# Layer 1 of a two-layer graph network: how a group's rows are finished, where head 0's and head 3's row sums are made, and which tiles take the log form

## The chip, the cores and the metric

The kernel runs on one core of one Trainium2 chip. The metric is the device time of one execution in microseconds, as the median of the runs; the profile is one further execution, taken by the hardware profiler. The core has five engines that run their own queues in order and wait for one another by semaphores: TensorE (PE in the profile; PEld is its weight load), VectorE (DVE), ScalarE (ACT), GpSimd (POOL) and SyncE (SP), which here only issues transfers.

## The reference

Two layers over 4096 nodes with 512 features. Layer 0 is a dense attention layer; the change does not touch it. Layer 1, with eight heads of 64 features, is this (the connectivity is the 0/1 matrix `adj`, added as it is):

```python
h = jnp.maximum(_layernorm(x, axis=-1), 0.0)
data1 = (h @ W.T + b).reshape(N, H, D)              # N, H, D = 4096, 8, 64
src = jnp.einsum('nhd,xhd->nh', data1, src_proj)
trg = jnp.einsum('nhd,xhd->nh', data1, trg_proj)
e = src.T[:, :, None] + trg.T[:, None, :]
e = jnp.where(e >= 0, e, 0.01 * e)
e = e + connectivity[None, :, :]
scores = jax.nn.softmax(e, axis=-1)
out = jnp.einsum('hnm,hmd->hnd', scores, data1.transpose(1, 0, 2))
x = x + out.transpose(1, 0, 2).reshape(N, H * D)
```

## The kernel before

Layer 1 works through eight groups. A group is a block `b` of 1024 target rows and a half `g` of four heads. Each group takes 32 steps; step `m` handles the source nodes 128m to 128m+127, which lie on the partitions, against the 1024 rows along the free axis. A head's unnormalised scores for one step are a 128x1024 product, called `pr` and numbered by head 0 to 3 within the half. The exponential of a leaky sum is written as a maximum of two factors times the exponential of `adj`, so that most products are one VectorE instruction.

The work of a step goes round the engines like this. SP loads a 128x1024 tile `e` of `adj` (L700, three buffers). ScalarE makes `ex` from it in PSUM (L718, one buffer) for heads 0, 1, 2, makes `e3` with a bias (L728) for head 3, and a rectified row `rl` for head 0 (L746). VectorE makes the four products in the order 3, 0, 1, 2 (`weigh`, L757 for head 0 and L760 for the others). The products of heads 1, 2 and 3 have two buffers each, those of head 0 three.

In `BY_LOG` steps head 0 is done in another form: ScalarE writes `lg` (L735), a GpSimd DMA adds `adj` to it (L736), and ScalarE's exponential gives the product (L743), so that VectorE has three products instead of four. These are the special tiles; before, they are steps 17, 21, 25 and 29.

TensorE's `gather` multiplies the products by the node values (L792). Each head's 64 features are split in two pieces of 32 columns, so four matmuls, each on its own 32 columns of the array, run side by side into the `pv` tiles. Row sums (the softmax denominators) go to `dn`, whose four quarters of 32 partitions are again four column tiles. Heads 1 and 2 have row sums on TensorE in every step. Head 0 has them on TensorE only in the steps that are not in `BY_DMA`; otherwise a GpSimd DMA adds the product to one of two accumulators `acc00`, `acc01` in SBUF (L774 to L776). Head 3's products are added up by a GpSimd `tensor_tensor` into `acc3` (L767, L769) for steps 0 to 30. A row sum of a single head 0 step fills only two of the four column tiles, so `side` switches between the two halves, and the next such step can use the other two. In the last step of a group TensorE adds the head 3 product of step 31 and the three accumulators, each once (L807 to L814). After that ScalarE copies `pv` to `os` (L821).

The group's end is spread over the next group's first steps by the generator `finish`: copy `dn` in step 0, turn the denominators in step 1 (L831), reciprocal `rd` on VectorE in step 2 (L835), and then one 128-row tile of the group per step: two transposes on TensorE (L847) into the one `pt` buffer, four scaled ScalarE copies in the next step (L871), and, for every second tile, a GpSimd DMA that adds the residual `x1` (L874) and three steps later a SP DMA to the output (L877).

The order of work around all this is the loop at L964 to L975: for each program step `s` it calls each stage for step `s + ahead` and then one `next(ending)`. Every engine's queue follows that order.

```python
stages = ((load, 3), (logs, 5), (exps, 1), (weigh, 1), (factors, 2), (scale, 2), (gather, 0))
```

So while TensorE gathers step s, VectorE weighs s+1 and SP loads s+3. The broadcast rows `z` of the next group (four DMAs of 512 KB, L695) and `u` are issued inside `load`. The last group is finished by `finish_last`, which keeps everything on chip.

Of the kernel before, what the change touches and what calls it, by code (L numbers as in the profile page):

```python
# [8 lines left out]
FP = mybir.dt.float32  # L9
AF = mybir.ActivationFunctionType  # L10
ALU = mybir.AluOpType
# [4 lines left out]
P = 128  # L16
# [12 lines left out]
def kernel(  # L29
# [15 lines left out]
    nc = tc.nc  # L45
    N, F = x.shape
    H, D = 8, 64
    HG, WL = 4, 1024
    WT = WL // P
    NT = N // P  # L50
# [12 lines left out]
    x1 = dram.tile([N, F], FP, name="x1")  # L63
# [36 lines left out]
    with tc.tile_pool(name="w0", bufs=1) as wp, tc.tile_pool(name="a0", bufs=2) as ap_, tc.tile_pool(  # L100
        name="a0s", bufs=8
# [144 lines left out]
    with tc.tile_pool(name="mx", bufs=1) as mxp, tc.tile_pool(name="b_a", bufs=6) as adjp, tc.tile_pool(  # L246
        name="b_e", bufs=4
    ) as esp, tc.tile_pool(name="b_m", bufs=2) as mkp, tc.tile_pool(name="b_s", bufs=2) as sp, tc.tile_pool(
        name="b_p", bufs=6, space=PSUM
# [56 lines left out]
        for n in range(-6, len(items)):  # L306
# [3 lines left out]
            if n >= 0:  # L310
                i, j, t = items[n]
# [9 lines left out]
    with tc.tile_pool(name="c_a", bufs=11) as adjp, tc.tile_pool(name="c_b", bufs=4) as ebp, tc.tile_pool(  # L321
        name="c_e", bufs=9
    ) as etp, tc.tile_pool(name="c_w", bufs=3) as wkp, tc.tile_pool(name="c_t", bufs=3) as atp, tc.tile_pool(
        name="c_m", bufs=2
    ) as mxp, tc.tile_pool(name="c_o", bufs=4) as iop, tc.tile_pool(name="c_s", bufs=2) as sp, tc.tile_pool(
        name="c_p", bufs=1, space=PSUM
    ) as p_o, tc.tile_pool(name="c_q", bufs=3, space=PSUM) as p_t, tc.tile_pool(
        name="c_r", bufs=1, space=PSUM
# [3 lines left out]
        src, pts, aj, mks, ex, at = {}, {}, {}, {}, {}, {}  # L332
# [112 lines left out]
        left, scale = [], {}  # L445
# [145 lines left out]
        pt = p_t.tile([P, BL], FP, name="pt")  # L591
# [44 lines left out]
    HV = WL // BL  # L636
    JT = BL // P
    Q = P // 4
    BY_LOG = (17, 21, 25, 29)
    BY_DMA = [m for m in range(2, NT - 5) if m % 4 != 1]  # L640

    with tc.tile_pool(name="p", bufs=2) as prp, tc.tile_pool(name="rl", bufs=2) as rlp, tc.tile_pool(
        name="io1", bufs=3
# [48 lines left out]
        def zload(i, k):  # L692
            b, g = groups[i]
            zs_[i, k] = (zp1 if i % 2 else zp0).tile([P, WL], FP, name=f"z{k}")
            nc.sync.dma_start(zs_[i, k], row_bcast(z_d, WL, (g * HG + k) * N + b * WL))  # L695

        def load(i, m):
            b, g = groups[i]
            e = ep.tile([P, WL], FP, name="e")
            nc.sync.dma_start(e, adj_t[m * P:(m + 1) * P, b * WL:(b + 1) * WL])  # L700
            ra[i, m] = e
            if i + 1 < len(groups) and m == 28:
                us[i + 1] = usp.tile([P, WL], FP, name="u")
                b, g = groups[i + 1]
                nc.sync.dma_start(us[i + 1], row_bcast(u_d, WL, g * N + b * WL))
            if i + 1 < len(groups) and m in (20, 22, 24, 26):
                zload(i + 1, ORDER[(m - 20) // 2])

        def scale(i, m):

# [38 lines left out]
        def weigh(i, m, order=ORDER):  # L749
            h = groups[i][1] * HG  # L750
            x_ = ex.pop((i, m))
            for k in order:
                if (i, m, k) in pr:
                    continue
                w = prp.tile([P, WL], FP, name=f"pr{k}", bufs=3 if k == 0 else 2)
                if k == 0:
                    nc.vector.scalar_tensor_tensor(w, rl.pop((i, m)), ngd_m[:, h // HG, m:m + 1], x_,  # L757
                                                   op0=ALU.subtract, op1=ALU.mult)
                else:
                    nc.vector.scalar_tensor_tensor(w, zs_[i, k], g_m[:, h + k, m:m + 1],  # L760
                                                   e3.pop((i, m)) if k == 3 else x_,
                                                   op0=ALU.max, op1=ALU.mult)
                pr[i, m, k] = w
            w = pr[i, m, 3]
            if m == 1:
                acc[i, 3] = acp.tile([P, WL], FP, name="acc3", bufs=1)
                nc.gpsimd.tensor_tensor(acc[i, 3], pr[i, 0, 3], w, ALU.add)  # L767
            elif 1 < m < NT - 1:
                nc.gpsimd.tensor_tensor(acc[i, 3], acc[i, 3], w, ALU.add)  # L769
            if m in BY_DMA:  # L770
                n = BY_DMA.index(m)
                if n < 2:
                    acc[i, 0, n] = acp.tile([P, WL], FP, name=f"acc0{n}", bufs=1)
                    nc.gpsimd.dma_start(acc[i, 0, n], pr[i, m, 0])  # L774
                else:
                    nc.gpsimd.dma_start(acc[i, 0, n % 2], pr[i, m, 0], accum_op=ALU.add)  # L776

        def gather(i, m):
            b, g = groups[i]
            last = m == NT - 1  # L780
            if m == 0:
                pv[i] = ([[p_v.tile([P, BL], FP, name=f"pv{c}{q}") for q in range(HV)] for c in range(2)],
                         p_v.tile([P, BL], FP, name="dn"))
            v, dn = pv[i]
            by_pe = [u for u in range(NT) if u not in BY_DMA]
            side = sum(u < m for u in by_pe) % 2
            for c, pair in enumerate(((3, 0), (1, 2))):
                for q in range(HV):
                    for r in (side, 1 - side):
                        k = pair[r]  # L790
                        for c0 in range(0, D, Q):
                            nc.tensor.matmul(v[c][q][r * D + c0:r * D + c0 + Q, :],  # L792
                                             va[:, m, g * HG + k, c0:c0 + Q],
                                             pr[i, m, k][:, q * BL:(q + 1) * BL], start=(m == 0), stop=last)

            def den(r, w, src, q, **fl):
                nc.tensor.matmul(dn[r * Q:r * Q + w.shape[1], :], w, src[:, q * BL:(q + 1) * BL], **fl)  # L797

            for r in (side, 1 - side):
                for q in range(HV):  # L800
                    hk = g * 2 + r
                    den(r * HV + q, d0_m[:, hk, m, :] if m else d0_0[:, hk, :], pr[i, m, r + 1], q,
                        start=(m == 0), stop=False)
            if m in by_pe:
                for q in range(HV):
                    den(side * HV + q, zo[:, 1 - side:3], pr[i, m, 0], q, start=False, stop=False)
            if last:  # L807
                for q in range(HV):
                    den(HV + q, zo[:, 1:3], pr[i, m, 3], q, start=False, stop=False)
                for q in range(HV):  # L810
                    den(q, zo[:, 1:3], acc[i, 0, 1], q, start=False, stop=False)
                for r, a in enumerate((acc[i, 0, 0], acc[i, 3])):
                    for q in range(HV):
                        den(r * HV + q, zo[:, 1:3], a, q, start=False, stop=True)  # L814
            for k in range(HG):
                pr.pop((i, m - 1, k), None)
            if last:
                os_ = [[osp.tile([P, BL], FP, name=f"os{c}{q}") for q in range(HV)] for c in range(2)]
                for c in range(2):
                    for q in range(HV):  # L820
                        nc.scalar.copy(os_[c][q], v[c][q])  # L821
                late[i] = os_, dn
# [15 lines left out]
        def share(rd, t, r):  # L838
            q, j = divmod(t, JT)
            k = ORDER[r]  # L840
            e, r4 = (0, (k - 1) * HV + q) if k in (1, 2) else (1, (HV if k else 0) + q)
            return rd[:, j, e, r4:r4 + 1]
# [7 lines left out]
        def part(ap, i, t, n):  # L850

            b, g = groups[i]
            t += b * WT
            return ap[t * P:(t + n) * P, g * HG * D:(g + 1) * HG * D].rearrange("(j p) (h d) -> p j h d", p=P, h=HG)

        def finish(i):


            dens = denominators(i)
            os_ = next(dens)  # L860
            yield
            next(dens)
            yield
            rd = next(dens)
            pts, os2 = {}, {}
            for t in range(WT + 4):
                if 0 < t <= WT:
                    if t % 2:
                        o = iop.tile([P, 2, HG, D], FP, name="o")
                    for r, k in enumerate(ORDER):  # L870
                        nc.scalar.activation(o[:, (t - 1) % 2, k, :], pts[t - 1][:, r, :], AF.Copy,  # L871
                                             scale=share(rd, t - 1, r))
                    if t % 2 == 0:
                        nc.gpsimd.dma_start(o, part(x1, i, t - 2, 2), accum_op=ALU.add)  # L874
                        os2[t] = o
                if t - 3 in os2:
                    nc.sync.dma_start(part(out, i, t - 5, 2), os2[t - 3])  # L877
                if t < WT:
                    pts[t] = p_t.tile([P, HG, D], FP, name="pt")
                    turn(os_, t, pts[t])  # L880
                yield

        def finish_last(i):

# [5 lines left out]
            os_ = next(dens)  # L890
            pts = [p_v.tile([P, HG, D], FP, name=f"pv{c}{q}") for q in range(HV) for c in range(2)]
            xs = p_x.tile([P, 4, HG, D], FP, name="ex")
            pts += [xs[:, n, :, :] for n in range(4)]
            for t in range(4):
                turn(os_, t, pts[t])
            next(dens)
# [64 lines left out]
        factors(0, 1)  # L961
        scale(0, 1)

        stages = ((load, 3), (logs, 5), (exps, 1), (weigh, 1), (factors, 2), (scale, 2), (gather, 0))  # L964
        for s in range(len(steps)):
            for f, ahead in stages:
                if s + ahead < len(steps):
# [44 lines left out]
```

## Time and profile before

| what | value |
|---|---|
| median of 3 runs | 2971.45 us (2970.3 to 2971.49) |
| the profiled execution's own time | 2974.0 us |
| its span, first to last instruction | 2972.2 us |
| layer 1's first and last `pv` matmul | 1743.5 us, 2956.0 us |
| granted TensorE clock | 0.996 |
| one VectorE product, 128x1024 (L760 on `ex`) | 1272 ns mean |
| one GpSimd sum, 128x1024 (L769) | 2410 ns mean, 232 of them |
| DMA accumulations of head 0 (L774, L776) | 152, 512 KB each |

Layer 1 is the last 41% of the span. A table of the eight groups is part of the prediction. In such a table, the busy time of PE counts a matmul as busy from its start to a modelled end, and several matmuls run side by side, so a PE that is busy all the time does not mean that it has no free columns. For VectorE, ScalarE and GpSimd busy time is the time an instruction ran, waits inside the instruction included.

### The profile page before, as it was taken

Reading aid. Unit: us, or ns where it says so; the run is one execution under the profiler, and the core shown is the slowest. Engines: PE = TensorE matmul, PEld = TensorE weight load, DVE = VectorE, ACT = ScalarE, POOL = GpSimd, SP = SyncE. Lnnn points to the kernel's source line nnn. Section 1 sums busy time; section 2 is a strip of 40 time slices with the busy share of each in tenths; the row PEclk is TensorE's granted clock in tenths of the full one; section 3 lists DMA queues with packets and bytes.
Section 4 is the critical chain, followed back from the end, with each engine's and each line's share of the span. In section 5 each row is a group of like instructions: output and inputs, shape, how many; then the busy total and the mean of one; then the engine's idle time right before and its main releaser. Section 6 shows DMA issues by size and latency. Waiting matters only on the chain.

```text
span 2972.2 us, 43109 instructions
## 1 busy us (share of the span) xinstructions
PE 2930.7 (99%) x15371; PEld 1159.4 (39%) x15371; DVE 2522.1 (85%) x3596; ACT 1326.1 (45%) x1852; POOL 1376.0 (46%) x1042
## 2 busy tenths in 40 slices
PE   8999999999999999999999989999999999999998
PEld 4444444444444444444444423323222322232222
DVE  5434777778888888888897789999999999999998
ACT  2121111111122122122122368888777777777776
POOL 3401111113444444444443656575757575757574
PEclk9999999999999999999999999999999999999999
DMA  4205666667976675665553149696969696979795
GB/s 155 96 7 179 223 222 219 230 219 184 208 180 172 159 177 173 157 175 177 155 179 99 54 138 239 183 255 192 251 196 247 201 248 202 241 206 240 209 230 154
DMA packets 454056, 552.02 MB, mean 186 GB/s; under 512 B 261624, under 2 KB 287256, under 8 KB 453840
## 3 DMA queue, kind: packets, MB, share of 16 engines
q1 hardware_dynamic: 400816, 387.81, 42.2%
q0 software_dynamic: 51008, 157.51, 23.0%
q10 hardware_dynamic: 2016, 3.93, 0.4%
q8 instruction: 121, 1.98, 0.3%
q14 instruction: 95, 0.78, 0.1%
HBM read 409.47 MB, written 59.97 MB: 158 GB/s over the span
## 4 chain that ended last, share of the span: by engine, by line
PE 85%; DVE 6%; DMA 4%; ACT 2%; issue 2%; POOL 1%; SPq 0%; DVEq 0%; ACTq 0%; POOLq 0%
PE po L437 30%; PE pv L792 20%; PE pe L288 15%; PE dn L797 7%; DVE pr L760 5%; PE ps L159 4%; PE po L507 4%; PE pe L166 4%; DMA acc<-pr 2%; DMA e<-in_adj_t_dram 1%; DVE pr L757 1%; PE pt L847 1%; ACT e L728 1%; POOL acc L769 1%; ACT ex L718 0%
## 5 line engine op out<-in xcount | busy, mean ns | idle before, releaser
L792 PE MATMUL pv<-pr,sup 128*32 128x512 f32 x8192 | 1010.4, 595 | 10.3 <-POOL d_m L957 5.4
L437 PE MATMUL po<-sup,at 128*128 128x512 f32 x2048 | 886.7, 594 | 2.2 <-DVE at L407 2.2
L769 POOL TENSOR_TENSOR acc<-acc,pr 128x1024 f32<-128x1024 f32 x232 | 559.2, 2410 | 315.4 <-DVE pr L760 314.9
L760 DVE SCALAR_TENSOR_TENSOR pr<-z,g_m,ex 128x1024 f32<-128x1024 f32 x512 | 630.7, 1272 | 7.9 <-ACT ex L718 7.5
L437 PEld LDWEIGHTS po<-sup,at 128*128 128x128 f32 x2048 | 387.4, 190 | 480.7 <-issue 446.1
L417 POOL TENSOR_TENSOR racc<-racc,ex 128x512 f32<-128x512 f32 x240 | 358.3, 1493 | 390.7 <-ACT ex L401 389.0
L792 PEld LDWEIGHTS pv<-pr,sup 128*32 128x32 f32 x8192 | 288.5, 110 | 594.6 <-issue 528.2
L401 ACT ACTIVATE ex<-d 128x512 f32<-128x512 f32 x256 | 160.5, 630 | 664.7 <-DVE d L399 648.1
L288 PE MATMUL pe<-he_t,he_t 128*128 128x512 f32 x896 | 386.4, 592 | 0.0
L718 ACT ACTIVATE ex<-e 128x1024 f32<-128x1024 f32 x256 | 263.0, 1027 | 219.7 <-DVE pr L760 219.4
L760 DVE SCALAR_TENSOR_TENSOR pr<-z,g_m,e 128x1024 f32<-128x1024 f32 x256 | 328.3, 1282 | 9.3 <-PE pv L792 5.4
L797 PE MATMUL dn<-pr,d_m 128*2 128x512 f32 x1984 | 335.4, 592 | 0.0
L728 ACT ACTIVATE e<-e,ld_m 128x1024 f32<-128x1024 f32 x256 | 291.3, 1138 | 17.7 <-DMA e<-in_adj_t_dram 17.5
L757 DVE SCALAR_TENSOR_TENSOR pr<-rl,ngd_m,ex 128x1024 f32<-128x1024 f32 x224 | 284.8, 1271 | 1.9 <-ACT ex L718 1.5
L746 ACT ACTIVATE rl<-z,ngd_m,d_m 128x1024 f32<-128x1024 f32 x224 | 275.1, 1228 | 0.0
L407 DVE TENSOR_TENSOR at<-ex,a 128x512 f32<-128x512 f32 x256 | 195.3, 763 | 80.0 <-ACT ex L401 51.2
L288 PEld LDWEIGHTS pe<-he_t,he_t 128*128 128x128 f32 x896 | 169.2, 190 | 210.1 <-issue 190.5
L291 ACT COPY es<-pe 128x512 f32<-128x512 f32 (+2 forms) x144 | 79.3, 551 | 377.0 <-PE pe L288 377.0
L292 POOL DMA_DIRECT2D e_d<-es x144 | 78.5, 545 | 364.7 <-ACT es L291 359.2
L399 DVE TENSOR_TENSOR d<-pt,mk 128x512 f32<-128x512 f32 x256 | 176.9, 691 | 8.8
L293 DVE CUSTOM_DVE_ANT_0 mk<-pe,mk 128x512 f32<-128x512 f32 (+2 forms) x144 | 93.0, 646 | 99.3 <-ACT es L291 99.3
L392 DVE TENSOR_SCALAR mk<-a 128x512 f32<-128x512 f32 x256 | 136.5, 533 | 1.9 <-DMA a<-in_adj_t_dram 1.9
(173 smaller groups left out, 2595.0 us busy)
## 6 DMA issues: line engine op xcount, KB each, us to landing
e<-in_adj_t_dram SPq DMA_DIRECT2D x256, 512.0 KB, 5.5
acc<-pr POOLq DMA_DIRECT2D x152, 512.0 KB, 5.8
a<-in_adj_t_dram SPq DMA_DIRECT2D x256, 256.0 KB, 3.3
ar<-in_adj_dram SPq DMA_DIRECT2D x120, 256.0 KB, 3.1
e_d<-es POOLq DMA_DIRECT2D x120, 256.0 KB, 3.1
eb<-e_d SPq DMA_DIRECT2D x456, 64.0 KB, 2.7
ac<-in_adj_t_dram SPq DMA_DIRECT2D x112, 256.0 KB, 3.6
et<-e_d SPq DMA_DIRECT2D x112, 256.0 KB, 3.4
```

The costliest lines, as they stand in the source:

```text
L288: nc.tensor.matmul(pe[:, :w], he_t[i][:, k, (t % TB) * P:(t % TB + 1) * P], he_t[j][:, k, BL - w:], start=(k == 0), stop=(k == KC - 1))
L407: nc.vector.tensor_tensor(w, e, aj.pop((b, m)), ALU.mult)
L417: nc.gpsimd.tensor_tensor(racc, racc, e, ALU.add)
L437: nc.tensor.matmul(po[j], w[:, j * P:(j + 1) * P], sup[:, m, :], start=(m == 0), stop=last)
L718: nc.scalar.activation(x_, ra.pop((i, m)), AF.Exp)
L728: nc.scalar.activation(x_, ra[i, m], AF.Exp, bias=ld_m[:, h // HG, m:m + 1])
L746: nc.scalar.activation(r, zs_[i, 0], AF.Relu, bias=ngd_m[:, h // HG, m:m + 1], scale=d_m[:, h, m:m + 1])
L757: nc.vector.scalar_tensor_tensor(w, rl.pop((i, m)), ngd_m[:, h // HG, m:m + 1], x_, op0=ALU.subtract, op1=ALU.mult)
L760: nc.vector.scalar_tensor_tensor(w, zs_[i, k], g_m[:, h + k, m:m + 1], e3.pop((i, m)) if k == 3 else x_, op0=ALU.max, op1=ALU.mult)
L769: nc.gpsimd.tensor_tensor(acc[i, 3], acc[i, 3], w, ALU.add)
L792: nc.tensor.matmul(v[c][q][r * D + c0:r * D + c0 + Q, :], va[:, m, g * HG + k, c0:c0 + Q], pr[i, m, k][:, q * BL:(q + 1) * BL], start=(m = ...
L797: nc.tensor.matmul(dn[r * Q:r * Q + w.shape[1], :], w, src[:, q * BL:(q + 1) * BL], **fl)
```

## The change

- Special tiles: `BY_LOG` becomes 8, 17, 22, 27, and `logs` is called six steps ahead instead of five.
- Head 0's row sums: `BY_DMA` has 20 steps (all of 2 to 30 without 4, 7, 10, 13, 15, 18, 20, 23, 25) in place of 19. Steps 0 and 1 are added by one GpSimd `tensor_tensor` into `acc00` in step 1. That leaves ten steps for TensorE in place of 13.
- Head 3: step 31 is added by GpSimd too, and TensorE's separate row sum of it goes.
- The `z` rows of the next group are loaded in steps 2 and 3, two each (in group 0: steps 22 and 23), in place of steps 20, 22, 24, 26.
- `finish` turns two row tiles at once into one `pt` tile, in steps 2, 5, 8 and 11; ScalarE scales the first in the step after and the second in the one after that, followed by the residual DMA. The output DMA comes two steps after the residual DMA, not three.
- `finish_last` uses the quarters of its `xs` tile in the order 0, 2, 1, 3.

```diff
-    BY_LOG = (17, 21, 25, 29)
-    BY_DMA = [m for m in range(2, NT - 5) if m % 4 != 1]
+    BY_LOG = (8, 17, 22, 27)
+    BY_DMA = [m for m in range(2, NT - 1) if m not in (4, 7, 10, 13, 15, 18, 20, 23, 25)]
...
-            if i + 1 < len(groups) and m in (20, 22, 24, 26):
-                zload(i + 1, ORDER[(m - 20) // 2])
+            m0 = 2 if i else 22
+            if i + 1 < len(groups) and m0 <= m < m0 + 2:
+                for k in ORDER[2 * (m - m0):2 * (m - m0) + 2]:
+                    zload(i + 1, k)
...
             if m == 1:
                 acc[i, 3] = acp.tile([P, WL], FP, name="acc3", bufs=1)
                 nc.gpsimd.tensor_tensor(acc[i, 3], pr[i, 0, 3], w, ALU.add)
-            elif 1 < m < NT - 1:
+                acc[i, 0, 0] = acp.tile([P, WL], FP, name="acc00", bufs=1)
+                nc.gpsimd.tensor_tensor(acc[i, 0, 0], pr[i, 0, 0], pr[i, 1, 0], ALU.add)
+            elif m > 1:
                 nc.gpsimd.tensor_tensor(acc[i, 3], acc[i, 3], w, ALU.add)
             if m in BY_DMA:
                 n = BY_DMA.index(m)
-                if n < 2:
-                    acc[i, 0, n] = acp.tile([P, WL], FP, name=f"acc0{n}", bufs=1)
-                    nc.gpsimd.dma_start(acc[i, 0, n], pr[i, m, 0])
+                if n == 0:
+                    acc[i, 0, 1] = acp.tile([P, WL], FP, name="acc01", bufs=1)
+                    nc.gpsimd.dma_start(acc[i, 0, 1], pr[i, m, 0])
                 else:
-                    nc.gpsimd.dma_start(acc[i, 0, n % 2], pr[i, m, 0], accum_op=ALU.add)
+                    nc.gpsimd.dma_start(acc[i, 0, 1 - n % 2], pr[i, m, 0], accum_op=ALU.add)
...
-            by_pe = [u for u in range(NT) if u not in BY_DMA]
+            by_pe = [u for u in range(2, NT) if u not in BY_DMA]
...
             if last:
-                for q in range(HV):
-                    den(HV + q, zo[:, 1:3], pr[i, m, 3], q, start=False, stop=False)
                 for q in range(HV):
                     den(q, zo[:, 1:3], acc[i, 0, 1], q, start=False, stop=False)
...
+            old = None
+            for t in range(0, WT, 2):
+                pt = p_t.tile([P, 2, HG, D], FP, name="pt")
+                for j in range(2):
+                    turn(os_, t + j, pt[:, j, :, :])
+                yield
+                o = iop.tile([P, 2, HG, D], FP, name="o")
+                for j in range(2):
                     for r, k in enumerate(ORDER):
-                        nc.scalar.activation(o[:, (t - 1) % 2, k, :], pts[t - 1][:, r, :], AF.Copy,
-                                             scale=share(rd, t - 1, r))
...
+                        nc.scalar.activation(o[:, j, k, :], pt[:, j, r, :], AF.Copy, scale=share(rd, t + j, r))
+                    if j == 0:
+                        if t:
+                            nc.sync.dma_start(part(out, i, t - 2, 2), old)
+                        yield
+                nc.gpsimd.dma_start(o, part(x1, i, t, 2), accum_op=ALU.add)
+                old = o
                 yield
+            yield
+            nc.sync.dma_start(part(out, i, WT - 2, 2), old)
+            yield
...
-            pts += [xs[:, n, :, :] for n in range(4)]
+            pts += [xs[:, n, :, :] for n in (0, 2, 1, 3)]
...
-        stages = ((load, 3), (logs, 5), (exps, 1), (weigh, 1), (factors, 2), (scale, 2), (gather, 0))
+        stages = ((load, 3), (logs, 6), (exps, 1), (weigh, 1), (factors, 2), (scale, 2), (gather, 0))
```

More of the change, by code (lines that the diff above doesn't have):

```diff
@@ L864, in finish @@
             rd = next(dens)
[L865 to L869, printed above, removed]
-                    for r, k in enumerate(ORDER):
-                        nc.scalar.activation(o[:, (t - 1) % 2, k, :], pts[t - 1][:, r, :], AF.Copy,
-                                             scale=share(rd, t - 1, r))
[L873 to L880, printed above, removed]
+            old = None
[6 more added lines that the diff above has]
+                for j in range(2):
+                    for r, k in enumerate(ORDER):
+                        nc.scalar.activation(o[:, j, k, :], pt[:, j, r, :], AF.Copy, scale=share(rd, t + j, r))
[5 more added lines that the diff above has]
+                old = o
                 yield
+            yield
+            nc.sync.dma_start(part(out, i, WT - 2, 2), old)
+            yield
         def finish_last(i):
```

## The prediction

> **What bounds the kernel now.** I read the page's shares and chain first, then the windows of the eight groups, then the timeline of TensorE, VectorE, ScalarE and GpSimd in group 4, and last the transfers' landing times. The page gives TensorE the chain and VectorE the next place:
>
> ```profile
> PE 2930.7 (99%) x15371; PEld 1159.4 (39%) x15371; DVE 2522.1 (85%) x3596; ACT 1326.1 (45%) x1852; POOL 1376.0 (46%) x1042
> PE 85%; DVE 6%; DMA 4%; ACT 2%; issue 2%; POOL 1%; SPq 0%; DVEq 0%; ACTq 0%; POOLq 0%
> ```
>
> The shares are means over two layers. The windows, one for each of groups 2 to 5 here, show the stage that changes (columns: length, then busy time and count of PE, PEld, DVE, ACT, POOL):
>
> ```profile
> 2052.70:2202.90 150.20, 150.20 (x1372) 44.38 (x1366) 148.60 (x126) 116.97 (x139) 95.08 (x57) 1.00 0.84 225
> 2202.90:2355.10 152.20, 152.08 (x1380) 46.69 (x1378) 149.57 (x126) 116.46 (x138) 95.17 (x57) 1.00 0.83 222
> 2355.10:2505.40 150.30, 150.30 (x1376) 43.93 (x1372) 148.75 (x126) 117.08 (x139) 95.17 (x57) 1.00 0.84 225
> 2505.40:2657.70 152.30, 152.06 (x1383) 46.25 (x1381) 148.94 (x126) 116.76 (x138) 95.18 (x57) 1.00 0.84 222
> ```
>
> TensorE never rests, but VectorE works 148.6 to 149.6 us of each 150 to 152. Whatever TensorE loses beyond some 2.5 us a group, VectorE does not follow. TensorE's timeline prices its parts:
>
> ```profile
> 2365.68 3.64 PE L792 MATMUL pv<-pr,sup 128*32 128x512 f32 x32
> 2369.14 1.04 PE L797 MATMUL dn<-pr,d_m 128*2 128x512 f32 x8
> 2370.11 0.44 PE L847 MATMUL pt<-ident,os 128*128 128x128 f32 x2
> 2370.48 3.64 PE L792 MATMUL pv<-pr,sup 128*32 128x512 f32 x32
> ...
> 2414.36 3.62 PE L792 MATMUL pv<-pr,sup 128*32 128x512 f32 x32
> 2417.80 1.04 PE L797 MATMUL dn<-pr,d_m 128*2 128x512 f32 x8
> 2418.65 3.62 PE L792 MATMUL pv<-pr,sup 128*32 128x512 f32 x32
> ```
>
> A plain step takes 2418.65 - 2414.36 = 4.29 us: ten sets of four matmuls at 0.43. A step with a turned row tile takes 4.80, so a turn costs 0.51, of which the second transpose is about 0.14 (0.44 less one transpose's 0.30). A head 0 row sum fills two column tiles for two sets, 0.86. Two on opposite sides share that; one that stands before a turn pays all of it: step 5, which has both, takes 5.64.
>
> ScalarE starts a tile each 4.77 us, in VectorE's pace of four products at 1.19:
>
> ```profile
> 2383.48 1.03 ACT L718 ACTIVATE ex<-e 128x1024 f32<-128x1024 f32 x1 [0.73 <-DVE pr L760]
> 2384.44 1.13 ACT L728 ACTIVATE e<-e,ld_m 128x1024 f32<-128x1024 f32 x1
> 2385.48 1.23 ACT L746 ACTIVATE rl<-z,ngd_m,d_m 128x1024 f32<-128x1024 f32 x1
> 2386.61 0.90 ACT L871 ACTIVATE o<-pt,rd 128x64 f32<-128x64 f32 x4
> 2388.25 1.03 ACT L718 ACTIVATE ex<-e 128x1024 f32<-128x1024 f32 x1 [0.73 <-DVE pr L760]
> ```
>
> So VectorE's 4.77 is slower than TensorE's plain 4.29; special tiles (3.58) and turns let it catch up. And GpSimd can stop it:
>
> ```profile
> 2282.09 2.73 POOL L769 TENSOR_TENSOR acc<-acc,pr 128x1024 f32<-128x1024 f32 x1
> ...
> 2283.97 1.94 DVE L760 SCALAR_TENSOR_TENSOR pr<-z,g_m,e 128x1024 f32<-128x1024 f32 x1
> ...
> 2285.83 1.27 DVE L757 SCALAR_TENSOR_TENSOR pr<-rl,ngd_m,ex 128x1024 f32<-128x1024 f32 x1
> ```
>
> The head 3 product, alone in reading two SBUF tiles, began 0.85 before a GpSimd sum ended (2284.82) and took 1.94 in place of 1.27.
>
> **What the Trainium skill says.** "SBUF — State Buffer", section "SBUF: two separate sides": VectorE with two SBUF inputs and GpSimd exclude each other for a whole instruction. The lines above agree: overlap less 0.18 is lost. "TensorEngine Tiling (Array Packing)", section "Key Properties": a change of tiling mode drains TensorE; the 0.51 for two short transposes agrees. "DMA: Bandwidth & Descriptors", section "Issuing engines are not separate DMA queues": all issuers share 16 engines; the trace agrees, an `e` load lands in 3.9 us when alone and up to 11.4 among `z`, `lg` and `acc`. "PSUM — Partial Sum Buffer", section "Terms": two engines may not use one bank at once; of this I use only the last part of the change.
>
> **The change part by part, TensorE.** Now, between two starts of step 2 (2365.68 to 2516.73): 32 x 4.29 = 137.3, eight turns 4.1, denominators in step 1 1.1, and half-filled sums 10 x 0.86 = 8.6 (steps 5 and 9 alone, eight more for the fuller side of the rest, the accumulators included). That is 151.1 of 151.05 measured. Afterwards: steps 4, 7 and 10 pay alone, each before a turn; from 12 to the next group's step 1 each side has five. 8 x 0.86 = 6.9. Four double turns at 0.51 + 2 x 0.14 = 0.79 are 3.2. Sum 148.5, 2.6 less.
>
> **VectorE.** It keeps 124 products; 148.7 busy. New on it:
> - Step 1's added sum. GpSimd starts `acc3` 1.46 after VectorE starts the step (2356.01 against 2354.55) and takes 2.39; the new sum follows at once and ends at 1.46 + 4.78 = 6.24. VectorE wants its next two-SBUF product at 4.77: 1.47 of overlap, less 0.18, costs 1.3. Bounds: 0, if the wait met another; 2.4, the whole sum. I take 1.25. Today nothing stands there: GpSimd is idle 2.3 us after `acc3`.
> - Special tile 8. The copies of the second pair fall into the same program step, and ScalarE needs 3.1 + 0.9 + 0.1 = 4.1 us, VectorE only 3.6: 0.4. In step 11 `logs(17)`, 1.06, follows a step with copies: 4.1 + 1.06 against 4.9: 0.3. Bounds for both together 0 to 1.5.
> - ScalarE's waits at special tiles for a DMA (2.05 at `pr L743` in group 5) go, since the `z` loads leave the crowded second half; I leave 0.15.
>
> 148.7 + 1.25 + 0.7 + 0.15 = 150.8; the wait of VectorE's first product for head 3's last row sum (0.3 to 0.7, `ACT os`) is gone and 0.3 of stretched products is counted in the odd groups only, so I take 150.5. That is 2.0 more than TensorE's 148.5: TensorE now waits, first at the turn in step 2 for VectorE's reciprocal, which today is done 0.9 us ahead of need. Its saving is mostly not cashed.
>
> **Edits at nothing.** Step 31's GpSimd sum ends some 1 us after TensorE begins step 31, needed 5 later. Head 0's DMA of step 30 lands 5 to 6 us after issue, about when step 31 starts; its sum is last in that step. Four `z` loads (2 MB) with `e` and one `acc` in two steps: at 1.91 us a transfer (17 landings in 32.5 us of group 5) the backlog reaches 3.8, so `e` takes 7.7 of the 9.5 us it has; the cover is `e`'s third buffer. SP then issues them 1.1 us each, ahead of the next `e`. In group 0, with steps 22 and 23 crowded, ScalarE's waits (1.9 us of VectorE time in steps 21 to 25) fall to about 1. The output store, now a step earlier, waits in SP's queue for the residual DMA, and `e` loads wait behind it: residuals land 8.5 to 12.9 us after VectorE starts the step, the next `e` is due at 10.7, late by 3 at worst; it has 3 to 4 spare.
>
> **Sum against the profiled span, 2972.2.** By VectorE's start of each group, groups 1 to 6 last 151.2 each. Group 0: -1.0. Six groups x (150.5 - 151.2) = -4.2, and +0.8 in group 1, where ScalarE also scales values (0.57 a step). Last group: VectorE's lead over TensorE at step 31 falls from 5.3 to 3.6, -1.8; one row-sum pair less, -0.9; `finish_last` -0.5 if VectorE and ScalarE stop taking turns at a bank (0 to 1.0). Sum -7.6: span 2964.6. The median lies 0.75 below that span: 2963.8; I say 2963.5.
>
> **Rivals.**
> - A, the added sum costs VectorE little and ScalarE is not late: VectorE at 149.1, TensorE at 148.5. Six groups x 2.1 more than nothing plus the rest as above: -12.6 - 4.2 = -17, 2954.5. For it: 1.5 us of ScalarE slack in plain steps. Against: the lock is seen in the trace.
> - B, the same time: new waits of 0.7 a group eat the gain, 2969. For it: VectorE is already 98% busy.
> - C, slower: the output store. `e` must be issued by 20.9 - 6.0 - 0.5 = 14.4 us after VectorE's step start, so from a residual that lands after 14.4 each further us stops VectorE for as long, three times a group. At 16 that is 1.6 x 3 x 7 = 34 less the 8: 2997; at 15.2 it passes +0.2%. Against: 12.9 is the latest seen. For it: `lg(17)` now falls into the same steps.
>
> **How the numbers follow.** Main case 0.50, A 0.20, B 0.15, C 0.15. The measurement tells 0.2%, 5.9 us, from no change: faster is below 2965.5. The main case's own range, from 0.6 us a group either way, is 2958 to 2969, two thirds of it faster. Faster: 0.33 + 0.20 = 0.53, rounded to 0.55; same 0.15 + 0.15 = 0.30; slower 0.15. The range takes in A and B and the first part of C: 2951 to 2974.
>
> **What would show it.** Right: VectorE's product after step 1's two sums takes 2.5 in place of 1.28; groups last 150.5; TensorE's transposes in step 2 wait for the reciprocal; ScalarE's `DMA acc` waits are gone. A is right if VectorE has waits and TensorE is full at 148.5. C is right if ScalarE waits for `e` in steps 8 to 16. Wrong altogether if groups last over 151.5 without such waits, or the double turn costs more than two.

## The result and the profile after

The changed kernel takes 2971.91 us (median of 12 runs, 2968.41 to 2976.94) against 2971.61 us for the kernel before (12 runs). The ratio is 1.0000, with a 95% interval of 0.9992 to 1.0007: no change, where 2963.5 was forecast as the likeliest. The profiled span is 2973.0 us (2972.2 before).

The page's shares and chain, as shown before:

```profile
PE 2915.0 (98%) x15243; PEld 1150.5 (39%) x15243; DVE 2531.2 (85%) x3596; ACT 1322.6 (44%) x1852; POOL 1425.6 (48%) x1066
PE 71%; DVE 14%; DMA 6%; ACT 6%; issue 3%; POOL 1%; SPq 0%; DVEq 0%; ACTq 0%; POOLq 0%
```

TensorE is busy 15.7 us less, and the span is no shorter. The chain shows why: PE's share fell from 85% to 71%, while DVE, DMA and ACT rose by 8, 2 and 4 points. The windows of groups 3 to 6 (length, then busy time and count of PE, PEld, DVE, ACT, POOL):

```profile
2205.70:2356.90 151.20, 148.84 (x1362) 43.61 (x1358) 149.73 (x126) 116.20 (x138) 101.11 (x60) 1.00 0.90 227
2356.90:2507.50 150.60, 148.64 (x1360) 43.76 (x1356) 149.68 (x126) 116.21 (x138) 101.26 (x60) 1.00 0.90 227
2507.50:2658.20 150.70, 148.63 (x1360) 43.78 (x1356) 149.65 (x126) 116.06 (x138) 101.13 (x60) 1.00 0.89 228
2658.20:2810.10 151.90, 149.30 (x1360) 43.44 (x1356) 149.82 (x126) 116.13 (x138) 101.24 (x60) 1.00 0.88 220
```

The two engines have changed places. TensorE, busy for all of an even group before, now rests 2.0 to 2.6 us in each, and VectorE is busy 149.7 of 150.6 us in group 4. TensorE's timeline at the start of group 4 shows two of its new rests (a bracket gives the idle time and what ended it):

```profile
2356.89 3.62 PE L796 MATMUL pv<-pr,sup 128*32 128x512 f32 x32
2361.36 1.07 PE L801 MATMUL dn<-pr,d 128*32 128x512 f32 x8 [0.85 <-ACT od L829]
2362.24 3.62 PE L796 MATMUL pv<-pr,sup 128*32 128x512 f32 x32
...
2373.18 0.66 PE L849 MATMUL pt<-ident,os 128*128 128x128 f32 x4 [1.04 <-DVE rd L837]
2373.76 1.50 PE L796 MATMUL pv<-pr,sup 128*32 128x512 f32 x12
```

It waits in step 0 for ScalarE's copy of `dn` and in step 2 for the reciprocal. Both come from queues that run in VectorE's pace; TensorE reaches them earlier than before.

VectorE's timeline in the same place, and GpSimd's, show the first thing that lengthened VectorE's path:

```profile
2357.21 1.27 DVE L762 SCALAR_TENSOR_TENSOR pr<-z,g_m,e 128x1024 f32<-128x1024 f32 x1
...
2362.26 2.19 DVE L762 SCALAR_TENSOR_TENSOR pr<-z,g_m,e 128x1024 f32<-128x1024 f32 x1
```

```profile
2358.63 2.39 POOL L769 TENSOR_TENSOR acc<-pr,pr 128x1024 f32<-128x1024 f32 x1 [7.14 <-DVE pr L762]
2360.98 2.39 POOL L771 TENSOR_TENSOR acc<-pr,pr 128x1024 f32<-128x1024 f32 x1
```

The added sum ends at 2363.37 (2360.98 + 2.39), 1.11 us after VectorE's head 3 product of step 2 has begun, and that product takes 2.19 in place of 1.27.

The second thing is in SP's queue. Here are its waits for the residual DMA (total, times, longest), first of the kernel before, where one line has all 28 stores, then after, where a group's last store has a line of its own:

```profile
SPq L877 <- DMA o<-x: 20.0, 16, 2.7
```

```profile
SPq L879 <- DMA o<-x: 152.3, 21, 8.4
SPq L885 <- DMA o<-x: 49.2, 7, 7.9
```

While SP waits with the output store, the `e` loads behind it are not issued. In the changed kernel 28 `e` loads, one behind each store, are issued 2.3 to 4.5 us after ScalarE has read the buffer they go to for the last time; in the kernel before none is later than 0.03 us. The chain of waits of the changed kernel, in group 2 (start, length, what):

```profile
2107.36 9.36 DMA o<-x
2116.72 0.02 issue
2116.73 0.39 SPq L879
2117.13 0.04 issue
2117.17 0.02 SPq L700
2117.19 0.04 issue
2117.23 8.01 DMA e<-in_adj_t_dram
2125.24 0.02 issue
2125.26 0.02 ACTq L730
2125.28 0.04 issue
2125.33 1.15 ACT e L730
```

The path runs from the residual's landing through the store to an `e` load and on to ScalarE. Its waits for `e` over the whole run grew from 17.5 us (22 times) before to

```profile
ACT e L730 <- DMA e<-in_adj_t_dram: 39.8, 35, 2.5
```

Of the 37 us of them outside group 0, 29 stand in steps 16 and 19 to 21, from the loads behind the third and the fourth store of a group on. ScalarE's waits for the accumulating DMA at a special tile are all but gone, from 7.1 us to 0.4; in their place VectorE waits 2.4 us in all, four times, until an accumulation of head 0 has freed a product buffer.

### The profile page after: what moved, and what is told of

The parts are those of the page before. It is cut to its first block, busy times and chain, and to the rows that moved or that the text cites. A ratio compares the mean times of both kernels' runs of the same rounds, so it can differ in the third digit from the quotient of the medians.

```text
span 2973.0 us, 42842 instructions
## 1 busy us (share of the span) xinstructions
PE 2915.0 (98%) x15243; PEld 1150.5 (39%) x15243; DVE 2531.2 (85%) x3596; ACT 1322.6 (44%) x1852; POOL 1425.6 (48%) x1066
## 4 chain that ended last, share of the span: by engine, by line
PE 71%; DVE 14%; DMA 6%; ACT 6%; issue 3%; POOL 1%; SPq 0%; DVEq 0%; ACTq 0%; POOLq 0%
PE po L437 30%; PE pe L288 15%; DVE pr L762 11%; PE pv L796 10%; PE po L507 4%; PE pe L166 4%; PE ps L159 4%; PE dn L801 3%; ACT e L730 3%; DMA e<-in_adj_t_dram 2%; DMA acc<-pr 2%; DVE pr L759 2%; ACT rl L748 1%; ACT ex L720 1%; DMA o<-x 1%
## 5 line engine op out<-in xcount | busy, mean ns | idle before, releaser
L796 PE MATMUL pv<-pr,sup 128*32 128x512 f32 x8192 | 996.1, 594 | 13.0 <-POOL d_m L962 5.4
L773 POOL TENSOR_TENSOR acc<-acc,pr 128x1024 f32<-128x1024 f32 x240 | 584.9, 2437 | 336.6 <-DVE pr L762 334.9
L796 PEld LDWEIGHTS pv<-pr,sup 128*32 128x32 f32 x8192 | 281.3, 110 | 620.0 <-issue 538.0
L762 DVE SCALAR_TENSOR_TENSOR pr<-z,g_m,e 128x1024 f32<-128x1024 f32 x256 | 335.4, 1310 | 0.2 <-ACT e L730 0.2
L801 PE MATMUL dn<-pr,d_m 128*2 128x512 f32 x1984 | 321.2, 592 | 0.0
L780 POOL DMA_DIRECT2D acc<-pr x152 | 142.0, 934 | 0.1
```

Of the source, the lines that this page charges most:

```text
L796: nc.tensor.matmul(v[c][q][r * D + c0:r * D + c0 + Q, :], va[:, m, g * HG + k, c0:c0 + Q], pr[i, m, k][:, q * BL:(q + 1) * BL], start=(m = ...
```

## The experiments

Theory 1: VectorE's path sets the length of a group, so TensorE's saving cannot be cashed as it stands, and the forecast gain went to `e` loads that wait behind the store. Theory 2: TensorE's path still sets the length, and its new waits in steps 0 and 2 ate its saving. Each time below is a median beside runs of the kernel before on the same chip; those took 2971.92 us for the first four experiments and 2971.8 us for the last four.

**The store one step later.**

```diff
                     if j == 0:
-                        if t:
-                            nc.sync.dma_start(part(out, i, t - 2, 2), old)
                         yield
+                    elif t:
+                        nc.sync.dma_start(part(out, i, t - 2, 2), old)
...
             yield
+            yield
             nc.sync.dma_start(part(out, i, WT - 2, 2), old)
```

> The changed kernel with the output store again three steps after its residual DMA. Theory 1 (VectorE's path sets the length of a group; the store, waiting in SP's queue for the residual, holds up the e loads behind it): ScalarE's waits for e outside group 0 fall from some 20 us to under 8, groups 2, 3 and 6 fall from 151.2 to 151.9 towards the 150.6 of group 4, time 2963 to 2967, against 2971.9 for the change. Theory 2 (TensorE's own path sets the length, and its new waits in steps 0 and 2, for the copy of dn and for the reciprocal, ate its saving): those waits stay, time 2971 to 2973.

Measured: 2966.94 us, ratio 0.9983 (0.9976 to 0.9991). SP's waits for the residual and ScalarE's waits for `e`:

```profile
SPq L880 <- DMA o<-x: 45.6, 21, 3.4
SPq L886 <- DMA o<-x: 13.9, 7, 3.2
```

```profile
ACT e L730 <- DMA e<-in_adj_t_dram: 13.9, 21, 1.6
```

TensorE's waits in steps 0 and 2 are as they were (those steps take 5.35 and 6.13 us in group 5, as in the changed kernel). Over the whole run, first of the changed kernel, then of this one:

```profile
PE dn L801 <- ACT od L829: 6.7, 7, 1.7
PE pt L849 <- DVE rd L837: 6.2, 6, 1.0
```

```profile
PE dn L801 <- ACT od L829: 6.5, 7, 1.7
PE pt L849 <- DVE rd L837: 6.2, 6, 1.0
```

Still 5.0 us are gained. So the store cost about 5 us, and those waits did not set the time. No `e` load is issued late any more: SP still waits for residuals, but no load is more than 0.03 us behind its buffer.

**Steps 0 and 1 summed by TensorE again.**

```diff
-                acc[i, 0, 0] = acp.tile([P, WL], FP, name="acc00", bufs=1)
-                nc.gpsimd.tensor_tensor(acc[i, 0, 0], pr[i, 0, 0], pr[i, 1, 0], ALU.add)
...
-                if n == 0:
-                    acc[i, 0, 1] = acp.tile([P, WL], FP, name="acc01", bufs=1)
-                    nc.gpsimd.dma_start(acc[i, 0, 1], pr[i, m, 0])
+                if n < 2:
+                    acc[i, 0, 1 - n] = acp.tile([P, WL], FP, name=f"acc0{1 - n}", bufs=1)
+                    nc.gpsimd.dma_start(acc[i, 0, 1 - n], pr[i, m, 0])
...
-            by_pe = [u for u in range(2, NT) if u not in BY_DMA]
+            by_pe = [u for u in range(NT) if u not in BY_DMA]
```

> The changed kernel with the row sums of head 0's steps 0 and 1 back on TensorE and no added GpSimd sum. Theory 1: VectorE gets back some 1.1 us in each group (its head 3 product of step 2 takes 1.28 in place of 2.19), TensorE's 0.86 more per group is within its waits: 2962 to 2966. Theory 2: TensorE pays 0.86 in each group: 2977 to 2980.

Measured: 2965.23 us, ratio 0.9975 (0.9965 to 0.9985). VectorE's two head 3 products at the same place of group 4 in this run:

```profile
2349.33 1.28 DVE L762 SCALAR_TENSOR_TENSOR pr<-z,g_m,e 128x1024 f32<-128x1024 f32 x1
...
2354.37 1.28 DVE L762 SCALAR_TENSOR_TENSOR pr<-z,g_m,e 128x1024 f32<-128x1024 f32 x1
```

More work for TensorE and less time: theory 2 falls here. The added sum cost some 6.7 us, about 0.9 a group. The profiles put it where it was looked for: VectorE's steps 0 to 3 are 0.96 to 0.98 us shorter here in each of groups 2 to 7. (This profile is of the fastest of the eight runs, 2960.73 us, so its whole length is not compared.)

**Both edits.**

> Both edits together. Theory 1: the two gains add until TensorE's 149.3 a group is met: 2955 to 2961. Theory 2: 2976 to 2980.

Measured: 2961.50 us, ratio 0.9965 (0.9953 to 0.9978), just above the range of theory 1. The gains of 5.0 and 6.7 come to 10.4 together. Groups 4 to 6 take 149.5 to 149.65 us, and TensorE's step 0 still takes 4.8 to 4.9 with the wait for `dn`. TensorE's own work, 148.5 and the 0.86 of the sum it took back, is within 0.3 us of that length again.

**How much less TensorE work is worth to the kernel before.** One edit to it: `if m in by_pe:` becomes `if False:`.

> The kernel before with all head 0 row sums of single steps left out on TensorE (13 pairs a group; head 0's denominators are incomplete), nothing else changed: TensorE has some 6 to 7 us less to do in each group. Theory 1: VectorE's path allows 1 to 2 us a group: 2956 to 2964. Theory 2, where TensorE's path is the length: 2915 to 2925.

Measured: 2960.45 us, ratio 0.9959 (0.9943 to 0.9974). Groups 3 to 5:

```profile
2196.10:2346.80 150.70, 148.04 (x1324) 45.30 (x1320) 149.04 (x126) 116.56 (x138) 95.23 (x57) 1.00 0.85 224
2346.80:2495.80 149.00, 147.12 (x1326) 47.36 (x1322) 148.53 (x126) 116.49 (x138) 95.20 (x57) 1.00 0.84 227
2495.80:2646.40 150.60, 148.09 (x1325) 45.46 (x1321) 148.63 (x126) 116.48 (x138) 95.27 (x57) 1.00 0.85 224
```

With all those sums gone, an even group is still 149.0, VectorE being busy 148.5 of it; an odd one is 150.6 to 150.7, with VectorE's waits at special tiles. That is the floor which VectorE's path sets under the old plan: 1.3 us below the kernel before in an even group, and 1.1 a group on the mean of groups 0 to 6.

**The z loads back in the second half.**

```diff
-            m0 = 2 if i else 22
-            if i + 1 < len(groups) and m0 <= m < m0 + 2:
-                for k in ORDER[2 * (m - m0):2 * (m - m0) + 2]:
-                    zload(i + 1, k)
+            if i + 1 < len(groups) and m in (20, 22, 24, 26):
+                zload(i + 1, ORDER[(m - 20) // 2])
```

> The changed kernel with the z loads of the next group back in steps 20, 22, 24 and 26. If moving them was of use: the loads crowd the second half again, ScalarE's waits for e and for acc grow from 40 us to over 50, 2974 to 2980. If it was not: 2970 to 2973.

Measured: 2976.13 us, ratio 1.0012 (1.0004 to 1.0019). ScalarE's waits for `e`:

```profile
ACT e L728 <- DMA e<-in_adj_t_dram: 50.9, 39, 4.8
```

Moving the loads was worth some 4 us in the changed kernel. It is the part of the change that paid.

**The old finish, one row tile a step.** The whole of `finish` as before, all else changed.

> The changed kernel with the old finish: one row tile a step, store three steps after the residual. Theory 1: what counts is the store, since TensorE has room for eight single turns: as e1, 2965 to 2969. If the double turns' saving of 0.9 us a group on TensorE were cashed: 2972 to 2976.

Measured: 2971.93 us, ratio 1.0000 (0.9992 to 1.0008): theory 1's number missed, 5.0 us above the first experiment. ScalarE's waits for `e` are small (11.2 us), so the store is not it. VectorE's timeline behind tile 8 in group 4 shows what is:

```profile
2394.93 2.47 DVE L762 SCALAR_TENSOR_TENSOR pr<-z,g_m,ex 128x1024 f32<-128x1024 f32 x2
2397.87 1.28 DVE L762 SCALAR_TENSOR_TENSOR pr<-z,g_m,e 128x1024 f32<-128x1024 f32 x1 [0.47 <-PE pv L796]
```

VectorE waits for TensorE to free a product buffer. Eight single turns in a row slow TensorE in steps 2 to 9, just where tile 8 lets VectorE run ahead, and its products have two buffers (head 0 three). Against the first experiment VectorE's steps 8 to 13 take 0.90 us longer in each of groups 2 to 7, and its steps before tile 8 the same. So TensorE's time is not free everywhere: where VectorE has the full lead that the buffers allow, TensorE holds it back. The double turns are worth their 5 us through that place. The 0.90 is also what they save TensorE in a group; whether the two are equal by more than chance was not tried.

**Special tiles at 9, 18, 23, 28.** On top of both edits, so that no special tile is weighed in a program step in which ScalarE also copies a row tile.

> The kernel of e3_both with the special tiles at 9, 18, 23, 28. Theory 1: VectorE's losses of 0.35 and 0.16 a group behind tile 8 and behind the log row of tile 17 go, and most of the 2.1 us of group 0's steps 3 and 4; TensorE's 149.3 is near: 2957 to 2961, against 2961.5 of e3_both. Else no difference.

Measured: 2956.68 us, ratio 0.9949 (0.9936 to 0.9961), 4.8 us less than without and just below the range, but mostly not by the losses that were to go. In group 0 VectorE's step 4, 6.41 us with tile 8, does take 5.04 here: with tile 8 the log row's DMA stands in GpSimd's queue in step 2 and pushes `acc3` onto VectorE's head 3 product, which took 2.91. Steps 21 and 24 of that group, now 5.68 and 5.95 in place of 4.77, give it back, and group 0 as a whole is 0.2 us shorter. The loss around the first special tile stays as well (in group 4 steps 8 and 9 took 8.69, steps 9 and 10 take 8.63). VectorE's waits for an accumulation of head 0 to free a product buffer are gone, and groups 1 to 6 are 3.4 us shorter together. These waits in the run of both edits:

```profile
DVE pr L759 <- DMA acc<-pr: 3.7, 7, 1.0
```

Here there is none. Why the later tiles spare VectorE these waits was not tried apart.

**The version that the experiments point to.** The store later, those tiles, and the first two products of head 0 brought in by DMA, which neither TensorE nor the GpSimd sum pays for:

```diff
-                acc[i, 0, 0] = acp.tile([P, WL], FP, name="acc00", bufs=1)
-                nc.gpsimd.tensor_tensor(acc[i, 0, 0], pr[i, 0, 0], pr[i, 1, 0], ALU.add)
+                for n in range(2):
+                    acc[i, 0, n] = acp.tile([P, WL], FP, name=f"acc0{n}", bufs=1)
+                    nc.gpsimd.dma_start(acc[i, 0, n], pr[i, n, 0])
...
-                if n == 0:
-                    acc[i, 0, 1] = acp.tile([P, WL], FP, name="acc01", bufs=1)
-                    nc.gpsimd.dma_start(acc[i, 0, 1], pr[i, m, 0])
-                else:
-                    nc.gpsimd.dma_start(acc[i, 0, 1 - n % 2], pr[i, m, 0], accum_op=ALU.add)
+                nc.gpsimd.dma_start(acc[i, 0, n % 2], pr[i, m, 0], accum_op=ALU.add)
```

> The changed kernel with the store three steps after its residual, the first two products of head 0 brought into acc00 and acc01 by two GpSimd DMAs in step 1 in place of the GpSimd sum, and the special tiles at 9, 18, 23, 28. Theory 1: no sum beside VectorE's head 3 product of step 2, no special tile in a program step with copies, TensorE at 148.5 and VectorE at some 149 a group: 2952 to 2958. Theory 2 (TensorE's waits of steps 0 and 2 are the price): those waits stay, 2965 or more.

Measured: 2952.42 us, ratio 0.9933 (0.9921 to 0.9946): 19.4 us faster than the kernel before, and faster than the changed kernel by as much. Groups 3 to 5:

```profile
2194.70:2343.30 148.60, 148.48 (x1364) 43.98 (x1360) 148.41 (x126) 116.24 (x138) 100.04 (x61) 1.00 0.94 239
2343.30:2491.80 148.50, 148.38 (x1360) 43.94 (x1356) 148.32 (x126) 116.09 (x138) 100.06 (x61) 1.00 0.93 237
2491.80:2640.40 148.60, 148.49 (x1360) 44.00 (x1356) 148.41 (x126) 116.28 (x139) 99.98 (x61) 1.00 0.93 238
```

Now both engines are full: the 2.6 us a group that the change took from TensorE are cashed once VectorE's path is as short.

## Why the prediction was right and wrong

The bound was read rightly. That VectorE would take TensorE's place, that TensorE's saving would mostly stay uncashed, and that TensorE would wait at the reciprocal in step 2, all came out. TensorE's price list held too: in the changed kernel a step with a double turn and a lone row sum takes 5.82 in place of the forecast 5.94, and TensorE's 148.5 a group is what it takes in the last version.

The size was off by 8.4 us of span (-7.6 forecast, +0.8 measured). The measured time lies within the stated range, but outside the main case's own 2958 to 2969; it is there because the range was drawn wide enough for rival B and the first part of C. Its size is B's, no change; its cause is in good part C's, the store. Term by term, by VectorE's start of each group:

| term | forecast | measured |
|---|---|---|
| start of layer 1 | 0 | +1.0 |
| group 0 | -1.0 | +0.7 |
| groups 1 to 6 | -3.4 | +2.2 |
| group 7 up to step 31 | 0 | +0.3 |
| VectorE's lead at step 31 | -1.8 | -2.6 |
| after step 31 | -1.4 | -0.7 |

- **The step that failed is among the "edits at nothing": "The output store ... has 3 to 4 spare".** A residual lands 7.8 to 14.4 us after VectorE starts the step, 12.7 in the middle, and the store held SP up each of the 28 times, by 6.1 to 8.4 us, not only at worst. The forecast's latest landing, 12.9, was not the latest of the kernel before either: there one of group 7 came after 14.4. A late load is then issued close to the next one and to the log row of a special tile; in group 2 two such `e` loads took 7.2 and 10.8 us to land, and the spare was counted with 6.0. Moving the store alone gave back 5.0 us. In that run's profile groups 1 to 6 are 4.1 us shorter than in the profile before, where 3.4 was forecast, so this term alone is as large as what the six groups missed. Rival C named the mechanism. It put a cost only on landings after 14.4, which none exceeded, and 34 us on landings at 16; what came was 5.0 us without that threshold being passed.
- **The added sum** was forecast at 1.25 us a group and costs 0.92 in its product, right in mechanism and nearly in size. The step before is longer by 0.27 too, but so it is in the second experiment, without that sum. The trace agrees with the Trainium skill's "SBUF — State Buffer", section "SBUF: two separate sides", once more: of 1.11 us of overlap 0.92 was lost.
- **Group 0** was mis-sized: the waits that were to fall by 1 us did, but steps 3 and 4 grew by 2.1 us with tile 8's log row ahead of them, which the working never costed. In the run with tile 9 in place of tile 8 they are 0.3 longer than before.
- **The special tiles' cost beside copies**, 0.7 forecast, is 0.35 and 0.19 a group.
- **`finish_last`**: nothing in place of -0.5. VectorE and ScalarE still take turns, in the same order and with the same waits to 0.01 us:

```profile
2965.26 0.85 DVE L914 SCALAR_TENSOR_TENSOR pr<-ex,rd,e 128x64 f32<-128x64 f32 x4
...
2966.21 0.93 ACT L911 ACTIVATE pr<-ex,rd 128x64 f32<-128x64 f32 x4 [1.07 <-DVE pr L914]
2967.17 0.86 DVE L914 SCALAR_TENSOR_TENSOR pr<-ex,rd,e 128x64 f32<-128x64 f32 x4 [0.72 <-ACT pr L911]
```

With the quarters in the order 0, 2, 1, 3 VectorE reads the first half of `xs` and ScalarE the second, and they still wait for each other, so sharing a half was not the reason. On the four separate `pv` tiles just before, the two start together (2963.39 both), though they write into one output tile as here. That the wait hangs on `xs` as one tile fits this, but was not tried.

- **The start of layer 1**, 1.0 us later, lies in layer 0, which the change does not touch; among the ten profiles it varies from 1740.3 to 1743.0 us. It is not explained further.

## What to carry to other kernels

Before counting an engine's saving, work out the path of the next busiest engine to the same tenth: with two engines within 2% of each other, a saving on one is worth no more than the other's slack, and the changes that make it must not lengthen the other. A transfer that waits in a queue for another transfer holds up everything behind it in that queue; give it one more step rather than rely on the spare of the loads behind, since a delayed load can meet the next burst, as here. And cost the first round of a loop by itself: what is free in the steady state may meet other work there.

## What was not expected of the hardware

A residual DMA of 256 KB into SBUF with addition took 7.6 to 9.9 us to land in the changed kernel, 8.7 in the middle, where it had taken from 4.1, 7.1 in the middle, before; a plain `e` load of twice the size landed in 3.7 us at the quickest. In each of groups 1 to 7 the log row's accumulating DMA of tile 22 took 10.7 to 11.2 us to land, and the `e` load issued 0.9 to 1.2 us after it 9.3 to 10.9.
